# A two-layer graph attention kernel: head 0's second product in seven products, logits and weight sums dealt anew in the aggregations, and the last head's turned tiles in another order

## The chip, the cores and the metric

The kernel runs on one core of one Trainium2 chip. The metric is the device time of one launch in microseconds (us). It is compared by medians over several runs; a profile is one further execution.

## What is computed

`x` has 512 nodes of 768 features; `src` and `dst` are 16,896 edges (8,192 random edges in both directions, and a loop at each node). Two graph attention layers follow each other: the first has 8 heads of 768 features, the second one head. At the end stand a residual and a layer norm. Cut from the reference:

```python
def gat_layer(x, W, a_s, a_d, b, edge_index, concat):
    h = (x @ W).reshape(n, H, C)
    alpha_s = jnp.einsum('nhc,hc->nh', h, a_s)
    alpha_d = jnp.einsum('nhc,hc->nh', h, a_d)
    e = jax.nn.leaky_relu(alpha_s[src] + alpha_d[dst], 0.2)
    m = jax.ops.segment_max(e, dst, num_segments=n)
    e = jnp.exp(e - m[dst])
    denom = jax.ops.segment_sum(e, dst, num_segments=n)
    alpha = e / (denom[dst] + 1e-16)
    out = jax.ops.segment_sum(h[src] * alpha[:, :, None], dst, num_segments=n)
    return out.reshape(n, H * C) + b

h = jax.nn.elu(gat_layer(x, W1, a_src1, a_dst1, b1, edges, True))    # 8 heads of 768
x = layernorm(x + gat_layer(h, W2, a_src2, a_dst2, b2, edges, True)) # 1 head of 768
```

## The kernel before, in words

The kernel doesn't gather by edges. It counts the edges between each pair of nodes into `cnt` (512 x 512, four tiles of 128 target nodes) and works on dense 512 x 512 matrices: with the logarithm of the counts added to the logits, an exponential of a row gives the attention weights. All tensors of size are 32-bit floats, and the multiplications run as such on TensorE.

**One head of layer 1** is four stages, and the heads are interleaved. While head h is aggregated and multiplied by W2, head h+1 gets its attention matrix, and head h+2 its projection:

1. *Projection* (`projection`, `project_by_thirds`): `HS[h] = x @ W1[h]`, 512 x 768 by 768 x 768.
2. *Logits and attention*: `half_logits` (L418) and `logits` (L424) make the source and target logits of a tile of nodes, each one VectorE operation over 128 x 768 with a sum. `row_out` (L622 to L628) turns the source logits into a row, writes it to DRAM and reads it back to all partitions. `lift` (L633, ScalarE), `leak` (L637) and `rank` (L642, VectorE; L646, the exponential, on ScalarE) make the matrix by tiles; `weigh` (L875 to L878) makes the reciprocal of the sum. `fold_count` (L659) prepares a tile of `cnt` once, in head 0.
3. *Turning*: each tile of the attention matrix is transposed into `PT`. `turn_out` (L892 to L897) copies the 32-bit halves apart on ScalarE and starts a transposing DMA on SP's queue; `turn_in` (L900) copies its result into `PT` on ScalarE. `turn` (L884, L885) does the same by four transposes on TensorE and one copy. The last head uses both: tiles 0 and 1 by DMA, 2 and 3 on TensorE.
4. *Aggregation* (`mixed`, L950 to L1001): `gT = elu(HS^T @ PT + b)`, transposed, 768 x 512. *Second product* (`second_by_thirds`): `h2 += g @ W2[h]`, 512 x 768 by 768 x 768, summed over the heads in `h2`.

**Fewer products.** Every large multiplication is split so that sums of blocks replace products. In *halves* (a 2 x 2 by 2 x 2 split, `product`, L409) seven products P1 to P7 stand for eight; each is twelve recorded matmuls of 384 columns. In *thirds* (2 x 3 by 3 x 3, `by_thirds`, L477) fifteen products stand for eighteen; each is eight recorded matmuls of 256 columns. Thirds need more sums ahead (of gT: L1073 and L1076; of W: L170, or accumulating DMAs from POOL, L133), and each product's result is added with its sign into the output: on VectorE (L490), as ScalarE's copy where an output block is written for the first time (L483), or through ScalarE's copy into a buffer and an accumulating DMA on POOL's queue (L487, L488). In halves, the left sums are four operations of 128 x 768 (`left`, L389 to L392; `left_sums`, L933 to L936) and the right ones two of 128 x 1152 (`right`, L401 and L402). Before the change head 0's projection, head 1's and head 2's are in halves and all others in thirds; all second products of heads 0 to 6 are in thirds.

**An aggregation** (`mixed`) runs over c = 0, 1, 2, the chunks c and 3 + c of the 768 features together. For each it issues seven products of 256 columns (L972) in the order P1, P6, P7, P2, P5, P4, P3; P2 goes into P1's bank, P4 into P7's and P3 into P5's, so each of those must wait until the bank has been read. VectorE's part per c: `u` (L982), `w` (L983), the far half of `zr` from P5 (L988), the near half from P4 (L991), `u` from P3 (L995), and the closing operation of each elu (L912); ScalarE: `u`'s copy (L976) and the elu steps (L909 to L911). Between them `mixed` calls other work from a list `fill`: one item ahead of L988, and a share of the rest after L995. In the last round `ends` (the sums of gT for P13 and P8, with which the second product starts) stand around L991.

```python
            some(1)                                               # before L988
            tt(zr[:, far_], part("P5"), w, op=ALU.subtract)       # L988
            ...
            tt(u, part("P3", over="P5"), u, op=ALU.subtract)      # L995
            some(-(-len(fill) // (2 * (HK - c) - 1)))
```

For heads 2 to 6, `fill` holds in this order the W sums P4 and P1, the source logits of tiles 0 and 1, `row_out`, and the target logits of tiles 0 and 1. With one item ahead of L988 and shares of two, one and one after L995, a source logit of 0.95 us stands ahead of L988 in chunk 1 and a target logit in chunk 2.

**What sets the order.** The schedule is written out by hand: each engine runs its instructions in the order in which the Python code issues them, and waits on semaphores for what it reads or overwrites. In the loop over h (from L1103), `plan` is a table of what is issued behind which product of a second product. Transposes, weights and rows share SP's queue, and all accumulating DMAs share POOL's. Weights of W2 lie in the "w1" buffers (`w1_rows`, `w1_halves`, profile names w1r and w1t), weights of W1 from head 1 on in "w2" (w2r, w2t). `load_second(h)` issues the ten loads and the additions of W2 for thirds; `load_w2` issues the seven loads and two additions for halves. PSUM has five banks for products (`mm`).

Of the kernel before, what the change touches and what calls it, by code (L numbers as in the profile page):

```python
# [37 lines left out]
def gat_pass(  # L38
# [17 lines left out]
    P = 128  # L56
# [47 lines left out]
    def load_w(W, h, slot, m):  # L104


        t1 = wpool.tile([P, HK, HALF], F32, name=f"{slot}t1")
# [3 lines left out]
        rows_ = wpool.tile([P, DC, D], F32, name=f"{slot}r")  # L111
# [389 lines left out]
    def second_by_thirds(h, A_, B_):  # L501
        return by_thirds(h2, A_, B_, ("P13", "P2", "P8", "P4", "P12", "P9", "P6", "P0", "P1", "P14", "P10", "P5", "P11", "P7", "P3"),
                         h == 0, ((1, 2), (0, 0), (0, 2)) if h + 2 < H else ((1, 2),))
# [446 lines left out]
    def mixed(h, A_, B_, fill, ends):  # L950
# [4 lines left out]
        def some(n):  # L955
            for f in fill[:n]:
                f()
            del fill[:n]

        for c in range(HK):  # L960
# [26 lines left out]
            some(1)  # L987
            tt(zr[:, far_], part("P5"), w, op=ALU.subtract)  # L988
            for f in behind[1:] + ends[:1] * (c == HK - 1):
# [3 lines left out]
            for f in ends[1:] * (c == HK - 1):  # L993
                f()
            tt(u, part("P3", over="P5"), u, op=ALU.subtract)  # L995
            some(-(-len(fill) // (2 * (HK - c) - 1)))
# [65 lines left out]
    def g_thirds(h):  # L1062
# [3 lines left out]
        ends = absent.rearrange("p t n -> p (t n)").bitcast(F32) if h else pass_.rearrange("p j n -> p (j n)")  # L1066
# [34 lines left out]
    behind, in_second, in_third = [sums2.pop("P2")], [], {}  # L1101
    attend = []
    for h in range(H - 1):  # L1103
        last = h + 2 == H
        if 0 < h and not last:
# [8 lines left out]
        G, gsums = g_thirds(h)  # L1114
        halves = [half_logits(h + 1, t) for t in ((0, 1) if h else (0, 1, 3))]
        besides[2:2] = [s_ for s_, _ in halves] + [lambda: row_out(h + 1)]
        later = [d_ for _, d_ in halves]
        first = behind if 1 < h else []
        if h < 2:
            later[1:1], behind = behind, []  # L1120
        finish = mixed(h, AA, BB, first + besides + later[:len(later) if h else 2], [gsums[p] for p in ("P13", "P8")])
        besides, behind = [], []
        if h == 0:
            load_w1(2)()
        if not last:
            load_a(h + 2, a_src1[h + 2], a_dst1[h + 2])
            attend = attended(h)
        pairs = second_by_thirds(h, G, B2)
        q = {}

        def score(t):
            q[t] = lift(h + 1, t)

        def scored(t):
            leak(q[t])
            rank(q[t], t)

        def out_by_dma(t):
            turn_out(q[t], t, weigh(q[t], t, scale=False))

        def sum_up(*names):
            return [gsums[p] for p in names]

        def of_b(*names):
            return [sums2.pop(p) for p in names if p in sums2]

        def at(f, *args):
            return [lambda: f(*args)]

        plan = {0: of_b("P6") + sum_up("P14") + finish[:1], 1: finish[1:] + of_b("P4") + sum_up("P12"), 2: sum_up("P9", "P7"),  # L1150
                3: sum_up("P1") + at(score, 0), 4: sum_up("P6"), 5: at(scored, 0) + at(score, 1), 6: of_b("P1") + sum_up("P10"),
                7: at(scored, 1) + at(score, 2), 8: sum_up("P5") + of_b("P3"), 9: at(scored, 2) + at(score, 3),
                10: sum_up("P11"), 11: at(scored, 3), 12: [], 13: sum_up("P3")}
        if h > 1:
            plan[0][1:1] = [plan[13].pop()]
        if h == 0:
            plan[3][0:0], plan[6][0:0] = later[2:3], later[3:]
        behind_it = {1: of_b("P7")}

        def also(n, *what):  # L1160
            plan[n] = plan.get(n, []) + list(what)

        if h == 0:
            for t, n in enumerate((4, 5, 7, 9)):
                plan[n][0:0] = at(fold_count, t)
        for n, f in zip((8, 10), in_second):
            also(n, f)
        if 0 < h and not last:
            for f in attend:
                also(13, f)  # L1170
        for n, (multiply, empty) in enumerate(pairs):
            if last and n == 14:
                turn(q[2], 2)
                weigh(q[3], 3)
                multiply(lambda: turn(q[3], 3))
                turn_in(1)
            else:
                multiply()
            for f in plan.get(n, []):
                f()  # L1180
            if last and n in (7, 9, 11):
                weigh(q[(n - 7) // 2], (n - 7) // 2)
                if n < 11:
                    turn_out(q[(n - 7) // 2], (n - 7) // 2)
            if last and n == 12:
                turn_in(0)
# [238 lines left out]
```

## Time and profile before

| | us |
|---|---|
| median of 3 runs (lowest to highest) | 640.18 (640.12 to 640.87) |
| the profiled execution | 640.64 |
| its span, first to last instruction | 638.8 |
| TensorE busy (98% of the span) | 624.4 |
| VectorE busy (82%) | 524.6 |
| ScalarE busy (52%) | 332.6 |
| GpSimd busy (25%) | 158.1 |

The granted clock of TensorE is 0.997 of full speed over the span. The stages around the change lie in the span like this: aggregation of head 0 from 81.0, its second product from 100.1, the projection of head 2 from 129.4, the aggregation of head 1 from 156.5 and its second product from 174.9; then heads 2 to 6 with a period of about 71; the last second product in thirds (head 6) from 530.4, and the last aggregation (`aggregate`, L918) from 559.25.

How to read it: a row of the timeline gives the start, the time from the start of the first to the end of the last instruction merged into it, engine, line, operation, output and inputs, and how many were merged. In brackets stands the idle time of that engine ahead of it, and what it waited for. PE is TensorE's multiplication and PEld its loading of weights; DVE is VectorE, ACT ScalarE, POOL GpSimd, SP the queue of SyncE. Ends of matmuls are modelled, so consecutive rows of PE overlap by a fraction of a microsecond; the distance of two starts is what counts.

### The profile page before, as it was taken

What the parts mean: (1) busy time and instruction counts of PE and PEld (TensorE: products, weight loads), DVE (VectorE), ACT (ScalarE), POOL (GpSimd) and SP (SyncE); (2) the same over time, 40 slices, a digit from 0 to 9 for tenths busy, and PEclk for the clock granted to TensorE, in tenths of its full rate; (3) what the DMA queues carried; (4) which work ended last, traced back from release to release, by engine and by line L of the source; (5) the groups of instructions that cost most, each with busy time, mean ns of one, the idle gap of its engine ahead of it and who ended that gap; (6) DMA issues with size and microseconds to landing.
All of it is one profiled execution on the core that took longest, in us unless ns stands there. A gap on an engine that the chain in (4) does not pass through costs nothing.

```text
span 638.8 us, 8535 instructions
## 1 busy us (share of the span) xinstructions
PE 624.4 (98%) x2761; PEld 482.4 (76%) x2761; DVE 524.6 (82%) x1119; ACT 332.6 (52%) x584; POOL 158.1 (25%) x183
## 2 busy tenths in 40 slices
PE   8999999999999999999999999999999999999995
PEld 5555587766888888888888888888888888745553
DVE  8979989978898888968897878967896879856675
ACT  5874775750658246651658146751757055543440
POOL 1310042133332233323333432313342302100000
PEclk9999999999999999999999999999999999999998
DMA  8993399999999997999899998999899993530122
GB/s 297 327 236 91 81 262 266 262 263 238 245 203 160 307 255 181 191 287 219 217 205 204 294 251 191 176 278 243 207 212 225 283 275 66 88 123 1 33 58 77
DMA packets 111088, 129.00 MB, mean 202 GB/s; under 512 B 41734, under 2 KB 92222, under 8 KB 110270
## 3 DMA queue, kind: packets, MB, share of 16 engines
q1 hardware_dynamic: 75406, 90.63, 45.3%
q0 software_dynamic: 35200, 37.17, 38.1%
q10 hardware_dynamic: 432, 0.59, 0.3%
q8 instruction: 24, 0.39, 0.3%
q14 instruction: 26, 0.21, 0.1%
HBM read 99.25 MB, written 2.90 MB: 160 GB/s over the span
## 4 chain that ended last, share of the span: by engine, by line
PE 90%; DVE 6%; ACT 2%; issue 1%; DVEq 0%; ACTq 0%
PE mm L477 44%; PE mm L972 19%; PE mm L409 15%; PE mm L918 3%; PE mm L1371 3%; PE held L409 2%; DVE h L490 1%; PE tr L739 1%; DVE hs L1073 1%; DVE q L637 1%; DVE q L642 1%; DVE scr L418 1%; PE bc L276 1%; PE held L605 1%; PE bc L739 1%
## 5 line engine op out<-in xcount | busy, mean ns | idle before, releaser
L483 ACT ACTIVATE hs<-mm 128x512 f32<-128x512 f32 x30 | 17.9, 596 | 88.5 <-PE mm L477 70.5
L972 PE MATMUL mm<-PT,hs 128*128 128x256 f32 x252 | 61.3, 379 | 0.0
L646 ACT ACTIVATE q<-q,nmax 128x512 f32<-128x512 f32 x32 | 23.1, 721 | 59.6 <-DVE nmax L642 59.6
L490 DVE TENSOR_TENSOR hs<-hs,mm 128x512 f32<-128x512 f32 x45 | 30.8, 685 | 27.6 <-PE mm L477 25.1
L972 PEld LDWEIGHTS mm<-PT,hs 128*128 128x128 f32 x252 | 47.8, 190 | 7.2 <-ACT u L976 0.3
L488 POOL DMA_DIRECT2D h<-pass x24 | 30.4, 1369 | 90.4 <-ACT pass L487 88.4
L490 DVE TENSOR_TENSOR h<-h,mm 128x512 f32<-128x512 f32 x63 | 43.0, 684 | 8.1 <-PE mm L477 6.7
L133 POOL DMA_DIRECT2D w1t<-in_L_gnn_W_dram x21 | 34.5, 1675 | 47.5 <-DMA w1t<-in_L_gnn_W_dram 44.3
L972 PE MATMUL mm<-pS,gS 128*128 128x256 f32 x168 | 43.1, 379 | 0.0
L477 PE MATMUL mm<-w1t,hs 128*128 128x256 f32 x168 | 40.2, 382 | 1.4 <-ACT pass L487 0.7
L900 ACT COPY PT<-zr 128x1024 uint16<-128x1024 uint16 x34 | 39.2, 1154 | 3.7 <-DMA zr<-pS 2.1
L477 PE MATMUL mm<-w1r,hs 128*128 128x256 f32 x168 | 40.0, 380 | 0.2 <-ACT h L483 0.2
L477 PE MATMUL mm<-w1r,gS 128*128 128x256 f32 x168 | 39.7, 379 | 0.0
L477 PE MATMUL mm<-w2r,gT 128*128 128x256 f32 x160 | 37.9, 385 | 0.0
L477 PE MATMUL mm<-w2r,xT 128*128 128x256 f32 x160 | 37.8, 379 | 0.0
L477 PEld LDWEIGHTS mm<-w1t,hs 128*128 128x128 f32 x168 | 31.5, 190 | 7.4 <-DVE h L490 1.9
L477 PEld LDWEIGHTS mm<-w1r,hs 128*128 128x128 f32 x168 | 31.7, 190 | 4.8 <-ACT h L483 0.6
L972 PEld LDWEIGHTS mm<-pS,gS 128*128 128x128 f32 x168 | 31.9, 190 | 4.3
L477 PEld LDWEIGHTS mm<-w1r,gS 128*128 128x128 f32 x168 | 31.9, 190 | 4.4
L477 PEld LDWEIGHTS mm<-w2r,gT 128*128 128x128 f32 x160 | 29.6, 190 | 6.6 <-DVE hs L490 3.0
L477 PEld LDWEIGHTS mm<-w2r,xT 128*128 128x128 f32 x160 | 30.4, 190 | 4.1
L133 POOL DMA_DIRECT2D w1r<-in_L_gnn_W_dram x14 | 16.7, 1196 | 63.4 <-DMA w1r<-in_L_gnn_W_dram 46.4
(273 smaller groups left out, 1525.2 us busy)
## 6 DMA issues: line engine op xcount, KB each, us to landing
w2r<-in_L_gnn_W_dram SPq DMA_DIRECT2D x48, 384.0 KB
w1r<-in_L_gnn_W_dram SPq DMA_DIRECT2D x43, 384.0 KB
w1t<-in_L_gnn_W_dram SPq DMA_DIRECT2D x28, 256.0 KB
gT<-xd SPq DMA_DIRECT2D x5, 1280.0 KB
h<-pass POOLq DMA_DIRECT2D x24, 256.0 KB, 5.9
w1t<-in_L_gnn_W_dram POOLq DMA_DIRECT2D x21, 256.0 KB, 5.8
w2t<-in_L_gnn_W_dram SPq DMA_DIRECT2D x15, 256.0 KB
w2t<-in_L_gnn_W_dram POOLq DMA_DIRECT2D x15, 256.0 KB, 6.6
```

Source lines behind the costliest of these rows:

```text
L133: nc.gpsimd.dma_start(o, i, accum_op=ALU.add)
L409: nc.tensor.matmul(ps[:, :HALF], A_[p][:, k, i * P:(i + 1) * P], B_[p][:, k, :], start=start and k == 0, stop=k == HK - 1, skip_group_chec ...
L477: nc.tensor.matmul(bank[chain][:, i * TH:(i + 1) * TH], A_[p][:, k, i * P:(i + 1) * P], B_[p][:, k, :], start=first and i == k == 0, stop= ...
L483: nc.scalar.activation(out(o), ps, AF.Copy, scale=sign)
L488: nc.gpsimd.dma_start(out(o), part, accum_op=ALU.add)
L490: nc.vector.tensor_tensor(out(o), out(o), ps, op=ALU.add if sign > 0 else ALU.subtract)
L646: nc.scalar.activation(q, q, AF.Exp, bias=nmax, scale=-1.0, accum_out=dens[t])
L739: nc.tensor.matmul(cps[t][r:r + B, :N], od[:, :, b - blocks[c][0], c // QC, c % QC], h_, start=todo[b] == hits[b], stop=todo[b] == 1, tile ...
L900: nc.scalar.copy(PT.rearrange("p s n -> p (s n)").bitcast(U16).rearrange("p (s n h) -> p s n h", s=NT, h=2)[:, :, t * P:(t + 1) * P, :], p ...
L918: nc.tensor.matmul(ps[:, :N], HS[h][:, s, c * P:(c + 1) * P], PT[:, s, :], start=(s == 0), stop=(s == NT - 1))
L972: nc.tensor.matmul(bank[p][:, :HN], A_[p][:, k, c * P:(c + 1) * P], B_[p][:, k, :], start=over is None and k == 0, stop=k == 1, skip_group ...
L1371: nc.tensor.matmul(ps[:, :cols.stop - cols.start], PT[:, s, t * P:(t + 1) * P], h2[:, s, cols], start=(s == 2), stop=(s == 1))
```

## The change

Head 0's second product is done in halves: `by_halves` is `projection` without its first two lines, and is now also called with `h2` as output, where P1 and P2 are copied by ScalarE and the other products are added by VectorE. Its weights come by `load_w2`, and its sums from `left` and `right`; the accumulating DMAs into h2 fall away in head 0. The table `plan` is not used for head 0; its steps are written out. All loads of W2 for head 1 come after head 0's last transposing DMA; the first two were issued in the middle of head 0's second product, the others after the last transpose.

`mixed` takes a table: for each chunk one list ahead of L988 and one behind L995. For heads 2 to 6, ahead of L988 stand a source logit (chunk 0), `row_out` (1) and the W sum P4 (2); behind L995 a source logit and the W sum P1 (0), a target logit (1) and a target logit (2). For head 1 they are: a source logit, `row_out` and the sum P8 of x; and a source logit, a target logit with the W sums P6 and P2, and a target logit. Head 0 keeps its order, but has three target logits at the end, of which one stood there and two in the second product, and no `ends`.

In the last head, `turn_in` of tile 1 is issued ahead of the copies of the tiles that are turned on TensorE instead of behind them, and tile 3 is weighted ahead of the addition of product 13.

```diff
@@ load_w
-        t1 = wpool.tile([P, HK, HALF], F32, name=f"{slot}t1")
+        t1 = w1_halves[1] if slot == "w1" else wpool.tile([P, HK, HALF], F32, name=f"{slot}t1")
...
@@ projection
-        HS[h] = hs = hpool.tile([P, NT, D], F32, name="hs")
+        HS[h] = hpool.tile([P, NT, D], F32, name="hs")
         new_alpha(h)
+        return by_halves(HS[h], XA, B_)
+
+    def by_halves(hs, XA, B_):
...
@@ mixed
-        def some(n):
-            for f in fill[:n]:
+        def some(c, j):
+            for f in fill[c][j]:
                 f()
-            del fill[:n]
...
@@ ahead of the heads
         if n == 10:
-            B2, sums2, load_pairs, load_first, load_rest = load_second(0)
-            load_pairs()
-            load_first()
-            load_rest()
+            load_w2(0, "w1")()
+            B2, pending = right(W2[0], "w1")
...
@@ head 0
+            GA, gsums = left(gT, gS)
+            finish = mixed(0, AA, BB, [[besides[:1], [besides[1], sources[0]]], [[sources[1]], [sources[2]] + row],
+                                       [besides[2:], list(targets)]])
             load_w1(2)()
+            load_a(2, a_src1[2], a_dst1[2])
+            attend = attended(0)
+            pairs = by_halves(h2, GA, B2)
+            for m, _ in pairs[:2]:
+                m()
+            pairs[0][1]()
+            for f in finish:
+                f()
+            gsums[0]()
+            pairs[1][1]()
+            gsums[1]()
+            pending[0]()
+            pairs[2][0]()
+            gsums[2]()
+            pairs[3][0]()
+            gsums[3]()
+            pending[1]()
+            pairs[2][1]()
+            pairs[3][1]()
+            fold_count(0)
+            score(0)
+            for n in range(2, 7):
+                (m0, e0), (m1, e1) = pairs[2 * n:2 * n + 2]
+                m0()
+                m1()
+                if n < 6:
+                    scored(n - 2)
+                if n < 5:
+                    score(n - 1)
+                if n == 6:
+                    turn_in(0)
+                    out_by_dma(2)
+                e0()
+                if 3 < n < 6:
+                    out_by_dma(n - 4)
+                if n == 6:
+                    out_by_dma(3)
+                    B2, sums2, load_pairs, load_first, load_rest = load_second(1)
+                    load_pairs()
+                    load_first()
+                    load_rest()
+                e1()
+                if n < 5:
+                    fold_count(n - 1)
@@ heads 1 to 6
+            amid = [[], of_b("P6", "P2"), behind] if h == 1 else [of_b("P1"), [], of_b("P4")]
+            finish = mixed(h, AA, BB, [[[sources[0]], [sources[1]] + amid[0]], [row, [targets[0]] + amid[1]], [amid[2], [targets[1]]]],
+                           [gsums[p] for p in ("P13", "P8")])
...
@@ the last head
                 if last and n == 14:
                     turn(q[2], 2)
-                    weigh(q[3], 3)
                     multiply(lambda: turn(q[3], 3))
-                    turn_in(1)
...
-                if last and n == 12:
-                    turn_in(0)
+                if last and n > 11:
+                    if n < 14:
+                        turn_in(n - 12)
+                    if n == 13:
+                        weigh(q[3], 3)
                 empty()
```

More of the change, by code (lines that the diff above doesn't have):

```diff
@@ L986, in mixed @@
             near_l = elu(h, c, part("P2", over="P1"), near, "l")
-            some(1)
+            some(c, 0)
             tt(zr[:, far_], part("P5"), w, op=ALU.subtract)
-            for f in behind[1:] + ends[:1] * (c == HK - 1):
+            for f in behind[1:] + list(ends[:1]) * (c == HK - 1):
                 f()
@@ L992, in mixed @@
             near_l()
[L993 removed]
+            for f in list(ends[1:]) * (c == HK - 1):
                 f()
             tt(u, part("P3", over="P5"), u, op=ALU.subtract)
[L996 removed]
+            some(c, 1)
             def others(c=c, u=u, zr=zr):
@@ L1156, in gat_pass @@
[L1156 to L1173, printed above, removed]
-                weigh(q[3], 3)
-                multiply(lambda: turn(q[3], 3))
-                turn_in(1)
-            else:
-                multiply()
-            for f in plan.get(n, []):
-                f()
[L1181 to L1184, printed above, removed]
-            if last and n == 12:
-                turn_in(0)
-            empty()
-            if not last and n == 13:
-                turn_in(0)
-            for f in behind_it.get(n, []):
-                f()
-            if last:
-                continue
-            if n in (7, 9, 11, 14):
-                out_by_dma(min(n - 7, 6) // 2)
-            if n == 5:
-                B2, sums2, load_pairs, load_first, load_rest = load_second(h + 1)
-                load_pairs()
-            if n == 14:
-                if 0 < h:
```

110 lines of the change are left out of this document (69 added, 41 removed).

## The prediction, made before the changed kernel was run

> **What bounds the kernel now.** I read the page first (busy shares, section 4), then the chain of waits in order of time, then the list of waits, then the timeline of the stages that the change touches. The page's chain by engine:
>
> ```profile
> PE 90%; DVE 6%; ACT 2%; issue 1%; DVEq 0%; ACTq 0%
> ```
>
> TensorE is busy for 624.4 of 638.8 us, so almost all that can be won is its 14.4 us of idle time, or fewer columns. The chain in order of time shows stages that are TensorE from end to end, beside others that should be:
>
> ```profile
> 129.55 27.09 PE mm L409 x84
> 156.64 18.38 PE mm L972 x84
> ...
> 299.01 18.63 PE mm L972 x84
> ```
>
> The first is a projection in 7 products with no gap, the price of one such multiplication: 27.09. The other two are the same 21 products of an aggregation, of head 1 and of head 3. In the timeline the gaps show. Of head 3, chunk 1 and the end of chunk 2:
>
> ```profile
> 308.86 0.95 DVE L418 SCALAR_TENSOR_TENSOR scr<-hs,a_s 128x768 bf16<-128x768 f32 x1
> 309.20 1.03 PE L972 MATMUL mm<-pS,hs 128*128 128x256 f32 x4
> 309.74 0.42 DVE L988 TENSOR_TENSOR zr<-mm,w 128x256 f32<-128x256 f32 x1
> 310.21 1.13 PE L972 MATMUL mm<-PT,gS 128*128 128x256 f32 x4
> 311.18 1.03 PE L972 MATMUL mm<-PT,hs 128*128 128x256 f32 x4
> ...
> 316.82 0.69 DVE L1076 SCALAR_TENSOR_TENSOR absent<-gT 128x512 f32<-128x512 f32 x1
> ...
> 317.57 0.92 PE L477 MATMUL mm<-w1t,absent 128*128 128x256 f32 x3
> ```
>
> A product follows the last after 0.865 when nothing waits. P3 is written into P5's bank and so waits until L988 has read it; L988 stood behind a 0.95 us logit, P3 starts 1.01 after P4 instead of 0.865, and the next product 0.97 after that. So chunk 1 takes 6.29 (304.89 to 311.18) where chunk 0 takes 6.05 (298.84 to 304.89). Chunk 2 has the same wait, and its late L988 also delays the sum L1076, for which the next stage waits: 6.39. The same chunk of head 1 has a 0.69 us sum (L1017) in that place instead of a logit:
>
> ```profile
> 172.78 0.69 DVE L1017 TENSOR_TENSOR xT<-xT 128x512 f32<-128x512 f32 x1
> 173.13 1.03 PE L972 MATMUL mm<-pS,hs 128*128 128x256 f32 x4
> 173.38 0.42 DVE L988 TENSOR_TENSOR zr<-mm,w 128x256 f32<-128x256 f32 x1
> 173.99 1.03 PE L972 MATMUL mm<-PT,gS 128*128 128x256 f32 x4
> ...
> 174.92 1.35 PE L477 MATMUL mm<-w1t,absent 128*128 128x256 f32 x5
> ```
>
> P3 comes 0.86 after P4, no wait, and the chunk takes 6.11 (168.81 to 174.92). In the list of waits, weight loads of L972 wait 13 times for L988: two chunks of heads 0 and 2 to 6, one of head 1. Head 0's second product and the last head's end:
>
> ```profile
> 100.13 1.99 PE L477 MATMUL mm<-w1t,pass 128*128 128x256 f32 x8
> 103.21 1.99 PE L477 MATMUL mm<-w1t,gT 128*128 128x256 f32 x8 [1.09 <-DVE w1t L170]
> ...
> 119.74 1.99 PE L477 MATMUL mm<-w1t,hs 128*128 128x256 f32 x8 [0.72 <-ACT pass L487]
> ...
> 124.10 1.99 PE L477 MATMUL mm<-w1t,hs 128*128 128x256 f32 x8 [0.18 <-DVE h L490]
> ...
> 129.38 0.81 PE L409 MATMUL mm<-w2r,xT 128*128 128x384 f32 x2
> ```
>
> ```profile
> 557.55 0.59 ACT L885 COPY PT<-tr 128x512 f32<-128x512 f32 x1 [1.20 <-PE tr L884]
> 558.03 1.16 ACT L900 COPY PT<-zr 128x1024 uint16<-128x1024 uint16 x1
> 559.25 3.27 PE L918 MATMUL mm<-PT,hs 128*128 128x512 f32 x7 [1.30 <-ACT PT L900]
> ```
>
> **Head 0's second product: 1.56.** It takes 29.25 (100.13 to 129.38). Fifteen products in thirds cost 15 x 8 records x 0.218 (52.32 by 240, head 3's stage behind its aggregation) = 26.16; the rest is waiting for VectorE, which is busy 28.1 of these 29.3. Seven products in halves cost 27.09, 0.93 more. VectorE loses eleven sums of gT, five W sums and six additions, all of 128x512 at 0.69 (15.2); it gets four sums of 128x768 (0.95, rows L933 to L936, one following at 0.86, or 1.06 if it needs the one before), two of 128x1152 (1.36, rows L401 and L402, the next at 1.27) and ten additions of 128x384 (0.55, rows L444 to L448, the next at 0.47), 12.0 in all.
>
> The start: without the two sums that ended the aggregation, and needing only gT's near halves of chunks 0 to 2, the first product follows P3 (99.07) at 0.96, at 100.03. VectorE's queue from there: u at 100.22, three target logits (0.33, then 0.99, 0.99, 0.88) to 103.41, the last two gT pieces (0.60, 0.45) to 104.46, two sums of gT (1.06, 0.86) to 106.38, the sum for P6 until 107.74. TensorE wants it at 100.03 + 4 x 1.935 (27.09 by the 14 halves of products) = 107.77: just in time. Then 0.86 + 0.86 of gT, 1.27 for P4's sum (from 107.65 to 110.64), count, leak and rank of tile 0 (0.60, 0.72, 0.69), two P6 additions (0.94), the same three for tile 1 (2.02) to 115.61, P7's first addition until 116.16. P4 goes into P7's bank and could start at 100.03 + 8 x 1.935 = 115.51, so it waits until 116.21: **0.70**, a stall that is new. Its bounds: nothing, if VectorE gets there 0.7 sooner; 1.3, if one operation of 0.60 later. I take the walk of the rows. Further on P3 needs P5's addition (123.34) by 123.95, which holds. End: 100.03 + 27.09 + 0.70 = 127.82, against 129.38.
>
> What hides the rest: ScalarE's copies of P1, which P2's bank waits for, stand behind the six elu activations of chunks 2 and 5 (3.15 from first to last, 100.44 to 103.59, now from 99.75), so the first is done at 103.4 against 103.90; past that each us costs one. The weights come by seven loads on SP (ten before) and two accumulating DMAs on POOL (eight before); the rows were in by 92.19, when POOL was released by them. An accumulation of 576 KB lands 7.2 to 15.6 after issue here, so at worst at 107.8; P7 reads it from 111.6. The projection behind begins with VectorE about 2.5 further behind than now (its three products with a_src2 and a_dst2 come after P3's last addition), and has 3.01 of idle time at 136.3 to take that in. Three DMAs into h2 are gone. SP's ten loads for head 1 now stand behind all four transposes, from about 129.5 instead of 117.33 and 134.18.
>
> **Aggregations: 2.84.** Heads 2 to 6: chunk 1 has the row's transpose (L622, 0.20) instead of a logit in front of L988: back to 6.05, 0.24 gained. Chunk 2 has a W sum of 0.68 (P4) where head 1 has L1017 of 0.69: 6.11 instead of 6.39, 0.28 gained. 5 x 0.52 = 2.60. Head 1: chunk 1 alone, 0.24. What moves in exchange lies beside TensorE: source logits at 301.97 in chunk 0, until 302.9, where L988 waits for TensorE until 303.36; a target logit behind chunk 1, where VectorE idles 1.26 before L982; in head 1 the logit joins two W sums there (0.88 more, against 0.17 of idle time), after which L982 and L983 come some 0.65 later than they could, still 0.9 ahead of P4, which waits for L983. Head 0's aggregation keeps its two logits. Should a gap stay, it costs the 0.24 or 0.28 that it costs now.
>
> **The last head: 1.05.** The aggregation's first product reads all of PT. Copy L885 of tile 3 ends at 558.14; then turn_in of tile 1 (L900) until 559.19. Moved ahead, it runs at 554.7 if its transpose has landed, and the product starts at 558.20. Tile 3 is weighted earlier too, which gains nothing: its turning comes after P3's sixth record anyway. The transpose was issued at 551.2. Alone, one landed in 2.8 (76.20 to 78.98), under a full load in 6.5 (132.20 to 138.71): 554.0 or 557.7, and here the DMA engines were idle from 556.5, so 556.8 at most. Until 555.85 the gain is whole; at 556.8 tile 1's copy pushes the two L885 to 559.04 and 0.15 is left. From 552.5 to 556.5 they moved 0.8 MB (0.2 per us); shared evenly with the accumulation beside it, the transpose's 0.26 are through 2.6 later, at 555.1. I take the whole gain.
>
> The Trainium skill ("DMA: Bandwidth & Descriptors", Queues, rings and completion order) says that a DMA engine takes turns between the queues with work, packet by packet. By that the transpose on SP's queue isn't held up by POOL's accumulation, and the sum stays; were POOL's queue served first, it would be 0.9 smaller. No row of before tells the two apart.
>
> **Sum.** 1.56 + 2.84 + 1.05 = 5.45. The profiled execution took 640.64 (span 638.8 and 1.84 around it): 635.19. It lies 0.46 above the median of 640.18, from which I forecast **634.7**. A measurement can tell 0.2% (1.3 us) from no change, that is below 638.9 or above 641.5.
>
> **Rivals.**
> 1. Tile 1 lands late in the last head (above): 0.15 instead of 1.05, 635.6. For it: DMA engines full until 556.5. Against: the even share. 13%.
> 2. VectorE stays the bound of head 0's second product: its queue has 0.03 in hand at P6. If P6, P4 and P3 each wait and the stage takes what it took, 636.3. Against: its work falls by 3.2 of 28.1. 12%.
> 3. The gaps of the aggregations stay in part or come back. If chunk 2's stay, 636.1; if the products behind wait for the same sums instead, 637.6. Against: head 1's chunk 2 has no gap, and its next stage is not behind. 8%.
> 4. Slower: head 1's W2 loads. Their SP issues and POOL additions are moved behind head 0's last transpose; the sums P6 and P2 read them in head 1's aggregation, at about 168.4, and a wait there holds L982 to L988 and so TensorE, us for us. It decides against the change if the pairs land after 168.4 + 5.45 = 173.9. Against: issued near 129.5, additions land after 5.8, so by 145. 5%.
> 5. It moves TensorE's waits only, and the end stays: 640.2. 4%.
>
> The forecast has 58%, by itself 633.9 to 635.5: the stall at P4 from 0 to 1.3, and 0.1 either way. With rivals 1 and 2 the range is 633.7 to 636.6. Faster 0.91 (forecast and rivals 1 to 3), same 0.04, slower 0.05.
>
> **What would show it.** Aggregations of heads 1 to 6 at about 18.2 from first product to the next stage; no wait for L988's successor in them, but two in head 0. Head 0's second product about 27.8, with one wait of 0.7 at P4 for VectorE and none for a DMA. The last aggregation released by a copy of a tile turned on TensorE. I am wrong if TensorE waits elsewhere in head 0, if the heads' 52.3 grows by what the aggregations lose, or if ScalarE waits for a transpose ahead of L885's.

## The result, and the profile after

| | before | after |
|---|---|---|
| median of 22 runs each (lowest to highest) | 640.95 (639.77 to 646.52) | 639.30 (636.77 to 641.30) |
| the profiled execution | 640.64 | 639.91 |
| its span | 638.8 | 638.0 |
| TensorE busy | 624.4 | 623.7 |
| mean granted clock | 0.997 | 0.995 |

The ratio is 0.9958, with a 95% interval of 0.9943 to 0.9972: faster by 1.65 us, where 5.5 were forecast. The 22 times of the changed kernel lie in two groups: 8 from 636.77 to 637.61 with a mean granted clock of 0.998, and 14 from 639.10 to 641.30 with 0.993 to 0.996. The profiled execution belongs to the second. The mean alone doesn't tell the groups apart everywhere, because it also holds the drop of the clock at the end of a run, behind the last matmul (from 635.2 of 638.0 in this profile).

Section 4 of the page, the chain by engine; DMA is new in it:

```profile
PE 87%; DVE 6%; DMA 3%; ACT 2%; issue 1%; SPq 0%; DVEq 0%; ACTq 0%
```

The chain of waits in order of time (start, us, engine, line):

```profile
296.93 18.13 PE mm L974 x84
315.06 52.29 PE mm L480 x240
...
546.98 7.34 DMA zr<-pS
554.35 1.16 ACT PT L903
555.51 0.98 ACT PT L888 x2
556.53 22.56 PE mm L921 x48
```

The first two rows are head 3: its aggregation takes 18.13 where it took 18.63, and the second product behind it 52.29 (52.32 before). That gain stays. The last four are the end of the last head: tile 1's transposing DMA took 7.34 from issue to landing, ScalarE copied tile 1 and then the two tiles turned on TensorE, and only then the last aggregation began, which took 22.56 for the same 48 products that took 20.87 before:

```profile
559.25 20.87 PE mm L918 x48
```

The same place in the timeline of ScalarE, with the idle time in brackets:

```profile
549.41 1.15 ACT L903 COPY PT<-zr 128x1024 uint16<-128x1024 uint16 x1
554.35 1.16 ACT L903 COPY PT<-zr 128x1024 uint16<-128x1024 uint16 x1 [3.79 <-DMA zr<-pS]
555.41 1.06 ACT L888 COPY PT<-tr 128x512 f32<-128x512 f32 x2
```

ScalarE waited 3.79 for tile 1, with two finished tiles in PSUM behind it. In the list of waits TensorE's longest is now

```profile
PE mm L921 <- ACT PT L888: 2.8, 1, 2.8
```

and the table by windows of 1 us (window; PE, PEld, DVE, ACT, POOL busy; granted clock; DMA share; GB/s) shows what came of it:

```profile
553.00:554.00 1.00, 0.70 (x5) 0.30 (x3) 0.26 (x1) 0.00 (x0) 0.00 (x0) 1.00 0.15 24
554.00:555.00 1.00, 0.00 (x0) 0.00 (x0) 0.50 (x2) 0.65 (x1) 0.00 (x0) 1.00 0.35 43
555.00:556.00 1.00, 0.00 (x0) 0.00 (x0) 0.00 (x0) 1.00 (x3) 0.00 (x0) 1.00 0.73 221
556.00:557.00 1.00, 0.47 (x1) 0.36 (x2) 0.00 (x0) 0.48 (x1) 0.00 (x0) 0.86 0.98 378
557.00:558.00 1.00, 1.00 (x2) 0.34 (x1) 0.00 (x0) 0.00 (x0) 0.00 (x0) 0.50 1.05 421
558.00:559.00 1.00, 1.00 (x2) 0.34 (x1) 0.00 (x0) 0.00 (x0) 0.00 (x0) 0.50 0.97 350
559.00:560.00 1.00, 1.00 (x3) 0.37 (x2) 0.00 (x0) 0.00 (x0) 0.00 (x0) 0.50 1.00 402
560.00:561.00 1.00, 1.00 (x4) 0.52 (x3) 0.00 (x0) 0.00 (x0) 0.00 (x0) 0.94 0.38 151
```

TensorE idles 2.83 (553.70 to 556.53), and then works some 3.4 us at half its clock, two or three matmuls begun per us in place of three or four. Everywhere else ahead of the layer norm the clock is whole.

**Where the time went.** Head 0's aggregation begins at 80.96 before and at 81.16 after, which is the time that the start took. From there to the first product of head 6's second product (530.42 and 526.22) it is 449.46 before and 445.06 after: 4.40 gained, what head 0 and the aggregations were to bring (1.56 + 2.84); that it fits to the hundredth is luck, as experiment 6 shows the two parts off by 0.04 and 0.06 in opposite directions. From there to the last aggregation (559.25 and 556.53) it is 28.83 before and 30.31 after: 1.48 lost, where 1.05 was to be gained. The half clock costs 22.56 - 20.87 = 1.69. With the start (0.20) and 0.3 behind the aggregation and around the span, that is 0.20 - 4.40 + 1.48 + 1.69 + 0.30 = -0.73, the difference of the two profiled executions.

So these theories had to be tested. **A**: two parts of the change bring what was forecast, and the last head's new order gives it back, because tile 1 isn't there. **A1**: it isn't there because the accumulating DMA of 576 KB, the last W2 sum on POOL's queue, takes the DMA engines ahead of it. **C**: the half clock is a consequence of TensorE's idle time. Each has its rival in the expectations.

### The profile page after: what moved, and what is told of

Same layout as the page of the kernel before. It is cut to its first block, busy times and chain, and to the rows that moved or that the text cites. A ratio compares the mean times of both kernels' runs of the same rounds, so it can differ in the third digit from the quotient of the medians.

```text
span 638.0 us, 8411 instructions
## 1 busy us (share of the span) xinstructions
PE 623.7 (98%) x2725; PEld 477.2 (75%) x2725; DVE 523.3 (82%) x1112; ACT 329.8 (52%) x579; POOL 146.2 (23%) x174
## 3 DMA queue, kind: packets, MB, share of 16 engines
q1 hardware_dynamic: 74718, 90.17, 45.3%
q0 software_dynamic: 33008, 35.46, 36.2%
## 4 chain that ended last, share of the span: by engine, by line
PE 87%; DVE 6%; DMA 3%; ACT 2%; issue 1%; SPq 0%; DVEq 0%; ACTq 0%
PE mm L480 40%; PE mm L974 18%; PE mm L409 16%; PE mm L921 4%; PE mm L1414 3%; PE held L409 2%; PE tr L742 1%; DMA zr<-pS 1%; DMA w2r<-in_L_gnn_W_dram 1%; DMA w2t<-in_L_gnn_a_dst_dram 1%; DVE h L493 1%; DVE q L645 1%; DVE q L640 1%; PE bc L276 1%; PE held L608 1%
## 5 line engine op out<-in xcount | busy, mean ns | idle before, releaser
L491 POOL DMA_DIRECT2D h<-pass x22 | 26.5, 1313 | 89.2 <-ACT pass L490 79.3
L493 DVE TENSOR_TENSOR h<-h,mm 128x512 f32<-128x512 f32 x57 | 38.9, 684 | 7.3 <-PE mm L480 6.8
L903 ACT COPY PT<-zr 128x1024 uint16<-128x1024 uint16 x34 | 39.2, 1154 | 5.8 <-DMA zr<-pS 5.2
L133 POOL DMA_DIRECT2D w1t<-in_L_gnn_W_dram x18 | 29.4, 1651 | 29.6 <-PE mm L409 26.8
L480 PE MATMUL mm<-w1t,hs 128*128 128x256 f32 x144 | 34.3, 381 | 0.5 <-DVE h L493 0.5
L480 PE MATMUL mm<-w1r,hs 128*128 128x256 f32 x144 | 34.2, 379 | 0.0
L480 PE MATMUL mm<-w1r,gS 128*128 128x256 f32 x144 | 34.0, 379 | 0.0
L978 ACT COPY u<-mm 128x256 f32<-128x256 f32 x21 | 7.8, 371 | 45.7 <-PE mm L974 45.7
L480 PEld LDWEIGHTS mm<-w1t,hs 128*128 128x128 f32 x144 | 27.1, 190 | 5.1 <-DVE h L493 1.3
L716 DVE TENSOR_SCALAR os<-nodes,idx 128x512 bf16<-128x512 f16 x104 | 29.1, 352 | 1.4 <-PE tr L742 1.4
L480 PEld LDWEIGHTS mm<-w1r,gS 128*128 128x128 f32 x144 | 27.4, 190 | 3.7
```

The source lines that it names most:

```text
L133: nc.gpsimd.dma_start(o, i, accum_op=ALU.add)
L480: nc.tensor.matmul(bank[chain][:, i * TH:(i + 1) * TH], A_[p][:, k, i * P:(i + 1) * P], B_[p][:, k, :], start=first and i == k == 0, stop= ...
L491: nc.gpsimd.dma_start(out(o), part, accum_op=ALU.add)
L493: nc.vector.tensor_tensor(out(o), out(o), ps, op=ALU.add if sign > 0 else ALU.subtract)
L716: nc.vector.tensor_scalar(o, nodes, idx[:, c:c + 1], None, op0=ALU.is_equal)
L903: nc.scalar.copy(PT.rearrange("p s n -> p (s n)").bitcast(U16).rearrange("p (s n h) -> p s n h", s=NT, h=2)[:, :, t * P:(t + 1) * P, :], p ...
```

## The experiments

Lines are those of each run's own kernel (L903 and L921 of the changed kernel are L900 and L918 of the kernel before). "Start" is the time from the first product of head 6's second product to the first of the last aggregation (28.83 before, 30.31 after); "landing" is that of tile 1, from the end of ScalarE's copy that it follows to its landing as ScalarE sees it. The kernel before had medians of 640.9 to 641.5 beside them.

### 1. The last head's old order

```diff
@@ the changed kernel
+                    weigh(q[3], 3)
                     multiply(lambda: turn(q[3], 3))
+                    turn_in(1)
...
-                if last and n > 11:
-                    if n < 14:
-                        turn_in(n - 12)
-                    if n == 13:
-                        weigh(q[3], 3)
+                if last and n == 12:
+                    turn_in(0)
```

> The changed kernel, but with the last head's order as it was (tile 1's turn_in behind the two copies of the tiles turned on TensorE, tile 3 weighted after product 13's addition). Theory A (the loss lies in that reorder alone; head 0 and the aggregations gain what their stages show, 4.2 to 4.3 us): about 636.6 against 640.95, the last aggregation starting 28.8 after the last second product, as in the kernel before, and no stretch at half clock. Theory B (the other two parts cost something later, as traffic or clock): 638.5 to 639.5.

Measured: 636.97 (635.85 to 639.44), ratio 0.994 (0.9913 to 0.9967), against 641.05. Theory A in the main: the two other parts bring 4.1 to the median, and by the medians the kernel is faster without the third than with it, though the intervals of the two ratios overlap. Two of the theory's marks missed. The start is 29.62, not the 28.83 of before: here too TensorE waited 2.08 for tile 1, whose landing took 7.62. And of the 8 runs 3 lie at 638.35 to 639.44 with a clock of 0.995 or 0.996; the profiled one, at whole clock until its end, is not among them.

### 2. The new order alone, in the kernel before

```diff
@@ the kernel before
-                    weigh(q[3], 3)
                     multiply(lambda: turn(q[3], 3))
-                    turn_in(1)
...
-                if last and n == 12:
-                    turn_in(0)
+                if last and n > 11:
+                    if n < 14:
+                        turn_in(n - 12)
+                    if n == 13:
+                        weigh(q[3], 3)
```

> The kernel before with the last head's new order alone. Theory A: slower than before. Tile 1's transpose lands about 7 us after its issue, the copies of tiles 2 and 3 wait behind it on ScalarE, and the last aggregation starts about 1.6 later than before (30.4 after the last second product), with up to 1.7 more where the clock then falls to half: 642.5 to 644.3. The forecast's own step: 1.05 faster, 639.9.

Measured: 641.35 (639.50 to 644.24), ratio 1.0004 (0.9982 to 1.0027): neither of the two; the edit by itself is worth nothing. ScalarE waited again, less long, since the landing took 6.34:

```profile
557.01 1.16 ACT L900 COPY PT<-zr 128x1024 uint16<-128x1024 uint16 x1 [2.79 <-DMA zr<-pS]
558.07 1.06 ACT L885 COPY PT<-tr 128x512 f32<-128x512 f32 x2
```

Start 29.31, TensorE idle for 1.83, and the aggregation took 20.87 at a whole clock. So the order loses up to half a microsecond by itself; the rest of the loss after the change is a later landing and the half clock.

### 3. The last W2 sum on VectorE

```diff
@@ the changed kernel
-            last_sum()
+            lo_, hi_ = W2[H - 1][:2]
+            nc.vector.tensor_tensor(lo_[:, :, R], lo_[:, :, R], hi_[:, :, R], op=ALU.add)
```

> The changed kernel, with the last accumulating DMA (576 KB into the last W2, issued about 1.5 us before tile 1's transpose) replaced by the same sum as one VectorE operation of 128x1152. Theory A1 (the transpose is late because it shares the DMA engines with that accumulation): ScalarE does not wait for tile 1, the last aggregation starts about 27.8 after the last second product, 635.6 to 636. Theory A2 (a transpose takes some 7 us in any case, or the two transposes hold each other up): nothing gained, 637 to 639.4.

Measured: 635.16 (634.49 to 635.71), ratio 0.9899 (0.9868 to 0.9930), some 0.4 better than expected. Theory A1, and the whole gain that was forecast. ScalarE's rows:

```profile
551.33 1.16 ACT L903 COPY PT<-zr 128x1024 uint16<-128x1024 uint16 x1 [1.05 <-DMA zr<-pS]
552.39 1.22 ACT L888 COPY PT<-tr 128x512 f32<-128x512 f32 x2
```

The landing took 4.47 (from 546.86) where it took 7.3, the copy of tile 1 is done before the two others are due, and the chain of waits runs through TensorE:

```profile
552.55 0.45 PE tr L887 x4
553.02 0.59 ACT PT L888
...
553.66 20.87 PE mm L921 x48
```

Start 27.54, clock whole. VectorE's sum takes 1.35, beside the aggregation.

### 4. Tile 1 turned on TensorE

```diff
@@ the changed kernel
+                if last and n == 13:
+                    turn(q[1], 1)
...
-                    if n < 11:
+                    if n < 9:
                         turn_out(q[(n - 7) // 2], (n - 7) // 2)
...
-                    if n < 14:
-                        turn_in(n - 12)
+                    if n == 12:
+                        turn_in(0)
```

> The changed kernel, with tile 1 of the last head also turned on TensorE (four transposes, 0.44, and a copy) instead of by a DMA, so that nothing behind it waits for a landing. Theory A: 0.44 more of TensorE and no wait, the last aggregation starts about 28.3 after the last second product, no stretch at half clock: 636.1 to 636.5. Theory B: 638.5 to 639.5.

Measured: 635.89 (635.11 to 636.68), ratio 0.9913 (0.9882 to 0.9945). Start 28.16: the four transposes and a wait that they bring cost 0.6 against experiment 3, and the loss is gone, with the accumulation left where it was. That is slightly better than the 636.1 to 636.5 expected. It is the waiting for tile 1 that costs, whatever makes it late.

### 5. TensorE kept busy while it waits

```diff
@@ the changed kernel, behind the last second product
+            warm = bc.tile([P, 512], F32, name="bc")
+            for _ in range(24):
+                nc.tensor.transpose(warm[:, :P], ident, ident)
```

> The changed kernel with 24 turnings of the identity added on TensorE behind the last head's second product, into a bank that nobody reads; 24 by 0.11 us (four took 0.44) are 2.6 us and fill the 2.83 us in which TensorE waited for tile 1. They take nothing away and should end before the copy of the last tile does. Theory C: the half clock comes from TensorE's idle time. Then the last aggregation starts some 30.3 us behind the start of head 6's second product as it did in the changed kernel (30.31), but takes 20.9 us and not 22.6, the granted clock stays at 1.00 there, all runs lie in the lower of the two groups, and the median is near 637.2 (3.7 us under the kernel before). Rival R: the half clock comes from something else at that time, the loads of x at some 400 GB/s for one. Then two runs of three still lie near 639.4, and the median with them.

Measured: 637.65 (637.46 to 638.33, 11 runs), ratio 0.993 (0.9903 to 0.9958). Theory C. In the chain tile 1 is as late as in the changed kernel and the start the same (30.24), but the aggregation takes 20.87:

```profile
546.46 7.26 DMA zr<-pS
...
555.93 20.87 PE mm L921 x48
```

The loads of x run beside it at the same rate, with the clock at 1.00:

```profile
556.00:557.00 1.00, 1.00 (x3) 0.52 (x4) 0.00 (x0) 0.00 (x0) 0.00 (x0) 1.00 1.00 378
557.00:558.00 1.00, 1.00 (x4) 0.46 (x3) 0.00 (x0) 0.00 (x0) 0.00 (x0) 1.00 0.98 329
```

All 11 runs lie in one group, 0.5 above the lower one of the changed kernel (637.65 against 637.2), as the kernel before was 0.5 slower beside them (641.46 against 640.95). In this trace the clock drops only at 630.8, behind the last matmul. So the half clock is what the idle time brings: 1.69 us in the one trace that has it. By the times it comes in two runs of three, where the groups differ by some 2.2 us (639.4 against 637.2); the 0.5 between these two figures was not read from a trace.

### 6. Head 0's second product in halves alone

```diff
@@ the changed kernel, heads 1 to 6 (the last head's order as in experiment 1)
-            amid = [[], of_b("P6", "P2"), behind] if h == 1 else [of_b("P1"), [], of_b("P4")]
-            finish = mixed(h, AA, BB, [[[sources[0]], [sources[1]] + amid[0]], [row, [targets[0]] + amid[1]], [amid[2], [targets[1]]]],
+            if h == 1:
+                fill = [[[sources[0]], [sources[1]] + row], [[targets[0]], of_b("P6", "P2")], [behind, [targets[1]]]]
+            else:
+                fill = [[of_b("P4"), of_b("P1") + [sources[0]]], [[sources[1]], row], [[targets[0]], [targets[1]]]]
+            finish = mixed(h, AA, BB, fill,
```

> The changed kernel with the aggregations' old deal of logits and sums in heads 1 to 6 and with the last head's old order; only head 0's second product in 7 products is left of the change. Theory A (head 0 brings what was forecast): 1.56 us under the kernel before, some 639.4 where that is at 641.0, and the difference from the run with the last head's old order (636.97) is the aggregations' 2.84 us, less what the half clock took there. Rival: head 0's gain is given back in its projection or in head 1, whose loads come later. Then it is within 0.5 us of the kernel before, and the aggregations bring over 4 us.

Measured: 640.57 (639.30 to 643.67), ratio 0.9976 (0.9948 to 1.0004), against 641.46; the interval holds the forecast 1.56 and also no gain. The trace is sharper: from the first product of head 0's aggregation (80.25) to head 6's second product (528.11) it takes 447.86, which is 1.60 less than before; of experiment 1, with the new deal, it takes 445.08 (80.03 to 525.11), another 2.78 less. So 1.60 for head 0 (forecast 1.56) and 2.78 for the aggregations (forecast 2.84), and nothing of either is given back up to there. The median shows only 0.9, between the theory and the rival; in the trace 0.5 goes at the last head, where the aggregation starts at 29.34 and not at 28.83.

### 7. The sum on VectorE, with the old order and in the kernel before

Two kernels: experiment 1 with the edit of experiment 3, and experiment 2 with it.

> The changed kernel with the last head's old order, and with the last W2 sum (128x1152) on VectorE in place of the accumulating DMA of 576 KB. Theory A1 (the new order brings its whole 1.05 us where the accumulation is out of tile 1's way): tile 1 lands before ScalarE is done with the second of the tiles turned on TensorE, the aggregation starts 28.5 to 28.8 us behind head 6's second product as in the kernel before (28.8), and the time is 1.0 to 1.3 us over that of the new order with the sum on VectorE (635.16), so 636.2 to 636.5. Rival: the order is worth nothing even then, and what that kernel gained came from VectorE's sum alone: 635.2, with the start at 27.5.

> The kernel before with the last head's new order, and with the last W2 sum on VectorE in place of the accumulating DMA; nothing else of the change. Theory A1: tile 1 lands 4.5 us behind its issue, as in the run of the changed kernel with that sum, and not 6.3 us as in the run with the new order alone (641.35); the aggregation starts 27.5 to 27.8 us behind head 6's second product and the time is 1.0 to 1.3 us under the kernel before, 639.7 to 640.0 where that is at 641.0. Rival: the half clock or another cost is behind the missing gain of the order alone; then it stays within 0.4 us of the kernel before.

Measured: the first 636.06 (635.82 to 636.55), ratio 0.9893 (0.985 to 0.9937), start 28.65; the second 639.67 (638.44 to 644.57), ratio 0.9963 (0.9935 to 0.9991), start 27.54. Theory A1 in both: with the accumulation out of the way the new order starts the aggregation 28.65 - 27.54 = 1.11 sooner, the 1.05 of the forecast with the little that tile 3's earlier weighting adds; the second kernel is 1.8 under the kernel before, where the order alone was worth nothing (experiment 2), though by the interval alone it could be 0.6. Tile 1's landing is not seen there: ScalarE copies it without a wait 3.3 behind the copy that it follows. The rows for the second are read at the last head only; its profiled execution took 643.03, and lost time at 519 to 523 to a sum of W2 that landed late.

### 8. The accumulation behind tile 1, and a third of it

```diff
@@ the changed kernel, first variant (whole[1] is tile 1's DMA buffer)
+            nc.gpsimd.memset(whole[1][:, :1], 0.0)
             last_sum()
@@ second variant
-            last_sum()
+            lo_, hi_ = W2[H - 1][:2]
+            nc.gpsimd.dma_start(lo_[:, :1, R], w2[(H - 1) * D + HK * P:(H - 1) * D + HK * P + P, R].rearrange("(k p) d -> p k d", p=P), accum_op=ALU.add)
+            nc.vector.tensor_tensor(lo_[:, 1:, R], lo_[:, 1:, R], hi_[:, 1:, R], op=ALU.add)
```

> The changed kernel, with one GpSimd instruction (a column of tile 1's DMA buffer is overwritten once its copy is done) ahead of the last W2 sum's accumulating DMA: the 576 KB start only when tile 1 has landed and been copied, and VectorE gets no work more. They are read by the second layer's projection some 20 us later. Theory A1 (the accumulation delays tile 1's transpose): tile 1 lands 4.5 us behind its issue, as in the run with the sum on VectorE, the aggregation starts 27.7 to 27.8 us behind head 6's second product, the clock stays whole, 635.2 to 635.6. Rival: in that run it was VectorE's sum, not the missing accumulation, that moved things; then the landing stays at 7.3 and the start at 30.3, near 639.

> The changed kernel, with a third of the last W2 sum (128x384, 192 KB) left to the accumulating DMA and two thirds (128x768) on VectorE. Theory A1 with the delay in proportion to the bytes ahead: the landing, 4.5 us with nothing and 7.3 us with 576 KB beside it, comes after some 5.4; ScalarE copies tile 1 and then the two others by 8.0 us after that issue, the aggregation starts 28.3 to 28.5 us behind head 6's second product, 635.9 to 636.2. Rival: any accumulation beside the transpose costs the whole delay: 7.3, 30.3 and near 639. Other rival: a small one costs nothing: 4.5, 27.6 and 635.2.

Measured: the first 635.22 (634.87 to 635.69), ratio 0.9908 (0.9888 to 0.9928), against 640.91; the second 635.39 (634.56 to 636.61), ratio 0.9908 (0.9887 to 0.9928). In the chain of the first:

```profile
546.40 4.70 DMA zr<-pS
...
553.31 20.87 PE mm L922 x48
```

Start 27.67, with the same DMA of 576 KB and no work more for VectorE: it was the accumulation ahead of the transpose, and not VectorE's sum. With a third of it the landing took 5.2 (547.06 to 552.29) and the start was 28.15: with 0, 192 and 576 KB beside it the landing took 4.5 to 4.7, 5.2 and 7.3, which is 0.3 to 0.5 us for each 100 KB. The start and the time of the second are better than expected (28.3 to 28.5, 635.9 to 636.2), and its time is closer to the first than its start says (0.5 later); six runs can't tell that apart.

### What happens in the DMA engines

Section 3 of the page prints bytes and packets by queue; the trace gives them for any window. Turning tile 1 by DMA is 1,056 packets of 0.26 MB (experiment 4 has 73,662 on q1 where the changed kernel has 74,718), the accumulation 400 of 0.59 MB (experiment 3 has 32,608 on q0 against 33,008). In the changed kernel SP issued the transpose at 546.98. From 547 to 550.6 the queues moved this (queue; packets, MB, share):

```profile
q0 software_dynamic: 371, 0.54, 96.2%
q14 instruction: 1, 0.01, 0.6%
```

and from 550.6 to 552:

```profile
q1 hardware_dynamic: 809, 0.21, 90.2%
q0 software_dynamic: 55, 0.06, 25.9%
```

q0 is POOL's queue, with the accumulation, and q1 SP's, with the transpose. For 3.6 us the transpose had not one packet, while q0 sent 371 of the 432 that it sent until the transpose had landed. The transpose's first packet came at 550.65, as the accumulation ran out. With no accumulation ahead of it the first packet comes 1.2 behind the issue (experiments 3 and 8). So the 576 KB cost the transpose a start that is 2.5 later, and that is nearly all of the 2.6 to 2.9 by which it lands later. Its last 134 packets came from 552.5 to 553.7, with few bytes in the table by windows above (0.15 of the engines in 553 to 554), and the landing is seen 0.65 behind the last one, at 554.35.

In each profile with both, tile 1 lands behind the accumulation: by the list of DMA issues that one takes 7.3 us from 544.53 in the changed kernel, to 551.8, and 7.7 from 548.21 in experiment 2, to 555.9, where tile 1 came at 557.01.

The trace of the kernel before has the same picture, and could have been asked ahead of the prediction. Tile 1's transpose was issued at 551.18; from 551.2 to 555:

```profile
q0 software_dynamic: 382, 0.56, 96.3%
q14 instruction: 1, 0.01, 0.5%
```

and from 555 to 556.75:

```profile
q1 hardware_dynamic: 1056, 0.26, 75.3%
q0 software_dynamic: 46, 0.05, 16.3%
```

The whole transpose lies behind 555.0, and its last packet comes at 556.54. With the 0.5 to 0.7 us from the last packet to the landing that the other traces show, it landed at some 557.1 (an estimate), where 555.85 was the bound for the whole gain and nothing is left of it at 557.1.

## Why the prediction was wrong, step by step

**Right: head 0's second product (1.56).** It takes 27.80 (100.22 to 128.02) where 27.79 was forecast, and by experiment 6 it brings 1.60. TensorE has one wait in it, at P4, as the walk through VectorE's queue had it, at 116.30 where 116.21 plus the start's 0.20 was forecast:

```profile
116.30 1.88 PE L409 MATMUL mm<-w1t,gT 128*128 128x384 f32 x5 [0.32 <-DVE h L448]
```

The bracket shows 0.32; against 8 products of 1.935 from 100.22 (115.70) the start is 0.60 late, where 0.70 was forecast. Rival 2 fell with this, and rival 4 too: neither head 0 nor head 1 shows a wait for a DMA on TensorE.

**Right: the aggregations (2.84).** Heads 2 to 6 take 18.13 each (18.11 forecast, 18.63 less 0.52). Head 1's takes 18.29 from its first product to the next stage's (155.11 to 173.40) where it took 18.45 (156.47 to 174.92), 0.16 of the 0.24 forecast. The list of waits has 3 weight loads waiting for L990 in place of 13, two in head 0 and a short one in head 1 (0.2), and the periods behind are not longer (52.29 against 52.33). Measured 2.78; rivals 3 and 5 fell.

**Wrong: the last head (1.05).** The step that failed is "shared evenly with the accumulation beside it, the transpose's 0.26 are through 2.6 later, at 555.1. I take the whole gain", and with it the bound: "here the DMA engines were idle from 556.5, so 556.8 at most". Tile 1 was to land 3.9, at most 5.6, behind its issue; it took 7.34, and 6.34 to 7.62 in the other runs with the accumulation. Both halves of the reasoning were faulty. The two transfers don't share the engines until the accumulation is nearly out: the transpose moved nothing for 3.6 us behind its issue (0 of its 1,056 packets, against 371 on the accumulation's queue), so it starts 2.5 us later than alone. And that the DMA engines look idle doesn't prove a landing: in the changed kernel the share fell to 0.04 at 552.5, with 134 packets of the transpose still to come, and the landing was seen 1.85 later.

In the kernel before no wait showed this, since its ScalarE came to tile 1 at 558.03 and never waited for it. The prediction's "No row of before tells the two apart" is wrong all the same: the packets by queue, above, do. Rival 1 named this place, with half of the delay, and so priced it at 0.9 lost instead of 2.5 (from -1.05 to +1.48). "ScalarE waits for a transpose ahead of L885's" stood among the prediction's own signs of being wrong, and is what ScalarE's timeline after the change shows (3.79).

The rule of the Trainium skill that was weighed there ("DMA: Bandwidth & Descriptors", Queues, rings and completion order: an engine takes turns between its queues by packets) stood behind the even share. The trace doesn't agree with it as it was applied: no turn went to the transpose until 550.65 in the changed kernel, and none until 555.09 in the kernel before. The traces don't show how a packet of the rule relates to the packets that the profile counts.

**Missing: the half clock (1.69 in the profile, some 2.2 in two runs of three).** No row of the prediction weighed what an idle TensorE costs beyond its idle time; the idle stretch ahead of the last aggregation was 1.30 in the kernel before, at whole clock. The Trainium skill ("TensorE: Matmul & The Clock Gate", Part 1: The HAM clock gate) gives a free-running window of about 3.4 us and says the clock is halved after at least one idle window. The length of the half-clock stretch here agrees (3.41 us), and so do the stretches at whole clock on both sides of it in this trace, 549.55 and 75.09 us, which are 161 and 22 times 3.413: the clock changes on a fixed grid. The condition doesn't agree: 2.83 of idle time were enough in the trace. They lay whole in one interval of that grid (553.30 to 556.72). In experiment 1's trace 2.08 were split by the grid into 1.49 and 0.59 (an estimate, counted back from the drop at its end), and the clock stayed whole. That would explain why only some runs are hit, 14 of 22 and 3 of 8 by their times, but no trace of a second such run was kept.

Without the faulty step the forecast holds: experiment 3 and the first variant of experiment 8, in which tile 1 is on time, take 635.16 and 635.22, 5.9 and 5.7 under the kernel before, where 5.5 was forecast for the change. They are faster than both kernels. Experiment 8's first variant needs the least: one instruction of 0.10 us on GpSimd.

**Left open.** Whether a plain DMA of the same bytes holds up the transpose as the accumulating one does was not tried. Why the transpose gets no packet while the accumulation runs is not known: its issue on SP took 2.12 in the changed kernel and 1.28 in experiment 3, so a part of the delay is there already, but the first packet came another 1.5 behind the end of that issue. That experiment 1's 3 slower runs had the half clock is argued from their times and mean clocks; there is no trace of them.

## What to carry to other kernels

Before an in-order engine is given a wait earlier in its queue, look for a row that shows that wait's end. Where the kernel before never waited for the transfer, its landing is not in the list of waits; ask for the packets of its queue in narrow windows then, because an engine share or a split by bytes is no substitute. Here a transpose on the path moved nothing until the accumulation issued 2.5 us ahead of it was nearly out: try to issue the large transfer behind the one on the path, if its reader is far away. Price an idle stretch of TensorE of some 2 to 3 us with the half clock that may follow (2.83 brought it in a trace; 1.83 and 2.08 did not), and look at the spread of the runs: two groups of times are a sign of it.

## What was not expected of the hardware

- TensorE's granted clock went to 0.50 for 3.41 us after 2.83 us without work, in the trace and, by the times, in 14 runs of 22. With 24 idle transposes in that stretch it stayed whole in the trace and, by the times, in all 11 runs. It changes on a grid of 3.413 us, counted from its first change.
- A transposing DMA of 0.26 MB landed after 4.5 and 4.7 us with no accumulation ahead of it, 5.2 with 192 KB and 6.3 to 7.6 with 576 KB, always behind the accumulation's end. Its first packet came 1.2, 1.5 and 3.6 to 3.7 us behind its issue, and 3.9 in the kernel before.
- Its packets don't come in one stretch. In the changed kernel 134 of 1,056 came from 552.5 to 553.7, when the DMA engines moved at most 40 GB/s; in experiment 3 the last 32 came from 549.5 to 550.7, under 10 GB/s; in experiment 8's first variant half of them came behind 1.8 us in which only some 25 came. The landing is seen 0.5 to 0.7 us behind the last packet.
